# Row gathers of a sparse graph-attention layer, each block's first one made to wait for the sums three blocks back

## The chip, the core and the metric

The kernel runs on one core of one Trainium2 chip. A core has a matrix engine (TensorE, PE in the profile; its weight loads are PEld), VectorE (DVE), ScalarE (ACT), GpSimd (POOL) and SyncE (SP), each with its own queue of instructions[...]. The metric is the device time of one execution in microseconds (us).

## The reference

Two graph layers on 3327 nodes with 512 features; `adj` is a sparse 3327 x 3327 matrix whose first nodes have by far the most neighbours.

```python
h = relu(layernorm(x))
x = x + adj @ (relu(adj @ (h @ W1) + b1) @ W2) + b2          # layer 0
h = relu(layernorm(x))
t = adj @ h                                                   # layer 1
attn_a = sigmoid(concat([t, h]) @ Wa.T + ba)
attn_b = sigmoid(concat([t, h]) @ Wb.T + bb)
hs = h @ W_sa
scores = (hs @ a_left)[:, None] + (hs @ a_right)[None, :]
e = where(adj != 0, exp(-leaky_relu(scores, 0.01)), 0)
x_a = (e / (sum(e, axis=1) + 1e-5)) @ hs
x_b = adj @ (h @ W_gcnb) + b_gcnb
x = x + sigmoid(attn_a * x_a + attn_b * x_b)
```

## The kernel before

The nodes are padded to 26 blocks of 128 (NB = 26). Layer 0 reads the whole matrix twice, in chunks of 512 columns: once for `acc_u` (L511), once for `acc_g` (L665). Beside it the kernel lists, for every block but the first, which neighbours its nodes have, and GpSimd gathers the matrix's entries for these lists into `ae`. Layer 1's input rows are written to `h_dram` (L588).

Block 0 holds the hubs, whose rows are nearly dense: its two sums (with `adj` and with `e`) are made over all 26 blocks of rows, in `acc_hub`, by `add_hubs` (L619 to L639). The last product of these is the `add(1, NB - 1, ...)` of L639.

All other blocks are sparse. Block i has `rooms[i]` rooms: 3 for blocks 25 to 23, 4 for 22 to 11, 5 for 10 to 6, then 6, 6, 7, 8 and 10 for blocks 5 to 1. A room takes two indirect DMAs from GpSimd (L139, called from `attend`), each of 128 rows of `h_dram` (520 floats a row), so that a block of r rooms takes 2r row gathers, 238 in all. They land in a ring of 16 buffers, `rows` and `hr`, each of which holds one room; a buffer is free again when the products that read it are done. The blocks are taken from 25 down to 1. For block i the order of the work is:

- `attend(i)`: the row gathers on POOL; for each room an add of the two score parts on DVE (L780), then maximum, leaky part, exponential (ACT) and mask (L784 to L208), by segments of at most four rooms; the sum of the exponentials (L789).
- on PE, behind the step before: `weigh` of the block two steps back (p_b L863, p_a L870), `turn` of the block one step back (transposes L823, copied to `tyT` by DVE, L838), `add_es`, and `sums(i)` (L809), eight products per room.
- `copy_out(i)`: two copies of the sums to `ty` on ACT (L882, L886), which `turn` will read; `finish` of the block two steps back: L725 to L744 on DVE and ACT, and the store.

`weigh` starts with the hubs' block 0 after `sums(25)`. Its weights `W_g_sb` are loaded at the beginning of the stage (L711). The order on each engine is fixed by `queued` (an instruction is issued after those named); it makes no semaphore waits. Waits come from the data, from the ring's buffers, and from `pace`, which makes an instruction wait for a product. `attend` paces the first gather of a block:

```python
lead = LEAD[i < NB - 8]                                # LEAD = 3, 4
if k0 + k + q == 0 and len(combined) >= lead:
    pace(gathered[0], combined[-lead])
```

`combined` is the list of the last product of each `sums`. When block i is attended, its last entry is that of block i+1. So the first gathers of blocks 25 to 23 are not paced, those of 22 to 18 wait for the sums of block i+3, and those of 17 to 1 for the sums of block i+4. On a block of four rooms the ring of 16 buffers asks for block i+4 too.

Of the kernel before, what the change touches and what calls it, by code (L numbers as in the profile page):

```python
# [21 lines left out]
NQ = P // GW  # L22
HALF = P // 2
ROW = 520
LEAD = 3, 4
EH = 8
SEG = 4
WAKE = 30
# [18 lines left out]
def kernel(  # L47
# [17 lines left out]
    nc = tc.nc  # L65
    NP, D = x.shape
    HID = W1.shape[1]
    NB = NP // P
# [69 lines left out]
    def gather(dst, table, rows, last):  # L138
        return nc.gpsimd.indirect_dma_start(  # L139
            out=dst, out_offset=None, in_=table,  # L140
            in_offset=bass.IndirectOffsetOnAxis(ap=rows, axis=0),
            bounds_check=last, oob_is_err=False,
        )
# [21 lines left out]
    def pace(g, matmul):  # L165

        tc.add_manual_dep(
            g.ins, matmul.ins.name,
            mybir.DependencyInfo(mybir.DependencyClass.Sync, mybir.DependencyReason.DATA),
            reason="pace",  # L170
        )
# [7 lines left out]
    def queued(*insts):  # L179

        behind = ExitStack()
        for inst in insts:
            if inst is not None:
                behind.enter_context(tc.issue_after(inst.ins))
        return behind
# [18 lines left out]
    def masked_exp(e, adj):  # L204

        nc.vector.scalar_tensor_tensor(e, e, SLOPE, e, op0=ALU.mult, op1=ALU.max)  # L206
        done = nc.scalar.activation(e, e, AF.Exp, scale=-1.0)
        nc.vector.scalar_tensor_tensor(e, adj, 0.0, e, op0=ALU.not_equal, op1=ALU.mult)  # L208
        return done
# [6 lines left out]
    with (  # L216
# [402 lines left out]
        def add_hubs():  # L619

            def add(k, i, s):
                nc.tensor.matmul(  # L624
                    acc_hub[k], s, hrow[i % NR][:, :D], start=(i == 0), stop=(i == NB - 1)
                )

            for i in range(NB):
                while i not in rows_made:
                    yield  # L630
                add(0, i, a_hub[:, i, :])
                if i not in e_hub:
                    make_e_hub()
                yield
                if i:
                    add(1, i - 1, e_hub[i - 1])
                    e_added.add(i - 1)
                    yield
            add(1, NB - 1, e_hub[NB - 1])  # L639

        e_hub, e_added, last_e = {}, set(), [None, None]

        def make_e_hub():

            i = len(e_hub)
            if i not in rows_made or i - len(e_added) >= EH:
                return
            e = e_hub[i] = hubp.tile([P, P], F32, tag="e_hub", name=f"e_hub_{i}", bufs=EH)
            scores(e, s_hub, hrow[i % NR][:, D : D + 1])
            last_e[0] = masked_exp(e, a_hub[:, i, :])  # L650
            if i == 0:
                last_e[1] = nc.vector.tensor_copy(es_hub, e)
            else:
                last_e[1] = nc.vector.tensor_tensor(es_hub, es_hub, e, ALU.add)

        late, hubs = iter(()), add_hubs()
        QUIET = 6
        for c in range(NCH):
# [86 lines left out]
        return read_a, read_b  # L745

    with tc.tile_pool(name="spw", bufs=2) as spw:
        gathered, combined = [None], []
        own = [
            spw.tile([P, 2, ROW], F32, tag=f"hr{k}", name=f"hr{k}", bufs=1) for k in range(10)  # L750
        ]
# [4 lines left out]
        def attend(i, seg):  # L756


            r = rooms[i]
            k0, k1 = seg  # L760
            n = k1 - k0
            if k0 == 0:
                taken[i] = {"es": spw.tile([P, 2, GW], F32, tag="es", name=f"es_{i}")}
            es = taken[i]["es"]
            s_l = s_left[i * P // CW][:, i % (CW // P), :].rearrange("p (q i) -> p q i", q=2)
            both = ae[i][:, 2 * k0 : 2 * k1, :]
            e = both[:, :, GW:]
            hr = taken[i][k0] = []
            for k in range(n):
                hr.append(next(pairs))  # L770
                for q in range(2):
                    f = first[i] + q * r + k0 + k
                    with queued(gathered[0]):
                        gathered[0] = gather(
                            hr[k][:, q, :], h_dram[:, :], row_h[:, f : f + 1], NP - 1
                        )
                    lead = LEAD[i < NB - 8]
                    if k0 + k + q == 0 and len(combined) >= lead:
                        pace(gathered[0], combined[-lead])
                nc.vector.tensor_tensor(  # L780
                    e.rearrange("p (q k) i -> p k q i", q=2)[:, k],
                    s_l, hr[k][:, :, D : D + 1].to_broadcast([P, 2, GW]), ALU.add,
                )
            nc.vector.tensor_scalar(e, e, LEAST_SCORE, None, op0=ALU.max)  # L784
            exp = masked_exp(e, both[:, :, :GW])
            part = es
            if k0:
                part = spw.tile([P, 2, GW], F32, tag="part", name=f"part_{i}_{k0}")
            last = nc.vector.tensor_reduce(  # L789
                part, e.rearrange("p (q k) i -> p q i k", q=2), axis=AX.X, op=ALU.add  # L790
            )
            if k0:
                last = nc.vector.tensor_tensor(es, es, part, ALU.add)
            return last, exp
# [98 lines left out]
        with queued(last_e[1]):  # L893
            for seg in segments(NB - 1):
                made = attend(NB - 1, seg)
# [22 lines left out]
        for i in range(NB - 2, 1, -1):  # L918
            with queued(*held):
                for seg in segments(i):  # L920
                    made = attend(i, seg)
            if i == NB - 2:
                some_logits(2, made[0])
            with queued(added):
                added, add_es, end = weigh(*weighing)
            b, ty, es = turning
            with queued(added):
                tyT, added, copied = turn(b, ty, False)
            with queued(added):
                added = add_es()  # L930
            held = [copied, *end()]
            weighing = b, tyT, es
            with queued(added):
                for seg in segments(i):
                    added = sums(i, seg)
            combined.append(added)
            ty, last = copy_out(i, taken[i]["acc"])
            held.append(last)
            turning = i, ty, taken[i]["es"]

        segs = segments(1)
        with queued(*held):
            attend(1, segs[0])
# [26 lines left out]
    with tc.If(over > 0):  # L970
        with (
# [25 lines left out]
            for c in range(NCH):  # L997
# [34 lines left out]
                for b in range(w // P):  # L1032
                    i = c0 // P + b
# [63 lines left out]
```

## Time and profile before

| | |
|---|---|
| four runs | 855.86, 857.12, 859.83, 859.48 us; median 858.3 |
| the profiled execution's own time | 861.97 us |
| its span, first to last instruction | 860.2 us |
| mean granted TensorE clock | 0.971 |
| start of the first row gather | 461.98 us |
| last row gather starts | 815.2 us |
| row gathers: number, median length of a row | 238, 1002 ns |
| PE busy, POOL busy | 797.6 us (93%), 512.9 us (60%) |

A row of POOL's timeline gives the start and the length of one gather as GpSimd's own work, and in brackets how long POOL stood idle before it and which event came last before it started. A row of PE may merge several products, with their number. Start times are counted from the first instruction of the span.

### The profile page before, as it was taken

The page shows a single profiled execution, that of the slowest core. Times are in us where ns is not written, and L with a number is a line of the kernel's source. Part 1 is how long each engine was busy: PE and PEld are TensorE (multiplying, and loading weights), DVE is VectorE, ACT ScalarE, POOL GpSimd, SP SyncE. Part 2 cuts the span into 40 slices and gives each one's busy share as a digit, 9 for nine tenths or more (in the row PEclk, how much of TensorE's full clock was granted, in tenths as well). Part 3 has the DMA queues.
Part 4 walks back from the last instruction along what each step waited for, and adds up shares of the span by engine and source line. Part 5 has one row for each costly group of instructions (what it writes and reads, how often), then busy time and mean ns, then how long its engine had stood idle before and what let it go on. Part 6 is the DMA issues. An engine that isn't in the chain of part 4 may idle for free.

```text
span 860.2 us, 12424 instructions
## 1 busy us (share of the span) xinstructions
PE 797.6 (93%) x3707; PEld 427.5 (50%) x3707; DVE 519.4 (60%) x1668; ACT 188.3 (22%) x396; POOL 512.9 (60%) x533
## 2 busy tenths in 40 slices
PE   9999899999798999999999499799999999999795
PEld 8774444444543444444454365456564555454354
DVE  6778899998645776586565465354453535344342
ACT  6770000000002233033042121122221212112112
POOL 2303666666677776676664766767676767677500
PEclk9999999999799899999999799899999999999898
DMA  7787998897688998999956668878877777877620
GB/s 243 241 282 217 314 311 241 278 284 225 172 268 278 318 325 297 314 319 299 314 176 222 179 184 238 242 195 227 227 218 222 207 230 206 230 198 209 181 68 29
DMA packets 108219, 202.82 MB, mean 236 GB/s; under 512 B 17489, under 2 KB 31344, under 8 KB 108144
## 3 DMA queue, kind: packets, MB, share of 16 engines
q1 hardware_dynamic: 72800, 124.40, 44.4%
q0 software_dynamic: 26656, 66.41, 29.5%
q10 hardware_dynamic: 8688, 11.15, 3.9%
q8 instruction: 31, 0.51, 0.3%
q14 instruction: 44, 0.36, 0.1%
HBM read 182.22 MB, written 20.55 MB: 236 GB/s over the span
## 4 chain that ended last, share of the span: by engine, by line
PE 72%; DVE 9%; DMA 7%; issue 7%; POOL 1%; ACT 1%; SPq 1%; another core or an unknown queue 0%; POOLq 0%; DVEq 0%; ACTq 0%
PE acc L809 13%; PE acc_u L511 13%; PE p_b L863 11%; PE acc_g L665 11%; PE p_a L870 10%; DMA a<-in_adjT_dram 4%; PE pu L293 3%; PE ptt L823 3%; DVE most L515 2%; DMA xb<-in_x_dram 2%; PE p_list L459 2%; PE acc_hub L624 1%; DMA hr<-h_rows,row_h 1%; PE px L580 1%; PE pt L285 1%
## 5 line engine op out<-in xcount | busy, mean ns | idle before, releaser
L139 POOL DMA_INDIRECT ae<-in_adjT_dram,row_a x238 | 254.5, 1069 | 166.2 <-issue 64.3
L139 POOL DMA_INDIRECT hr<-h_rows,row_h x150 | 155.1, 1034 | 67.8 <-issue 34.7
L511 PE MATMUL acc_u<-a,rows 128*128 128x512 f32 (+1 forms) x364 | 167.3, 589 | 1.9 <-issue 1.2
L665 PE MATMUL acc_g<-a,g 128*128 128x512 f32 (+1 forms) x364 | 159.0, 575 | 8.1 <-DMA a<-in_adjT_dram 8.0
L139 POOL DMA_INDIRECT rows<-h_rows,row_h x88 | 90.9, 1033 | 53.1 <-issue 19.5
L863 PE MATMUL p_b<-W_g_sb,tyT 128*128 128x257 f32 x416 | 103.8, 396 | 16.9 <-issue 16.0
L515 DVE TENSOR_REDUCE most<-a 128x16 f32<-128x512 f32 (+1 forms) x182 | 112.1, 643 | 7.6 <-DMA a<-in_adjT_dram 4.3
L665 PEld LDWEIGHTS acc_g<-a,g 128*128 128x128 f32 x364 | 69.0, 195 | 87.0 <-issue 64.8
L863 PEld LDWEIGHTS p_b<-W_g_sb,tyT 128*128 128x128 f32 x416 | 78.7, 194 | 50.6 <-issue 24.9
L870 PE MATMUL p_a<-W_sa_sb,tyT 128*128 128x512 f32 (+2 forms) x216 | 94.7, 581 | 0.8 <-issue 0.8
L809 PE MATMUL acc<-hr,ae 64*64 64x512 f32 x600 | 86.5, 614 | 4.1 <-issue 3.4
L511 PEld LDWEIGHTS acc_u<-a,rows 128*128 128x128 f32 x364 | 65.6, 197 | 49.5 <-issue 43.2
L838 DVE COPY tyT<-ptt 128x512 f32<-128x512 f32 x51 | 34.9, 686 | 64.8 <-PE ptt L823 26.4
L870 PEld LDWEIGHTS p_a<-W_sa_sb,tyT 128*128 128x128 f32 x216 | 41.2, 191 | 40.8 <-issue 39.2
L809 PE MATMUL acc<-rows,ae 64*64 64x512 f32 x352 | 53.6, 596 | 3.3 <-DVE ae L206 1.9
L809 PEld LDWEIGHTS acc<-hr,ae 64*64 64x64 f32 x600 | 35.3, 137 | 39.3 <-issue 37.5
L208 DVE SCALAR_TENSOR_TENSOR ae<-ae 128x256 f32<-128x256 f32 (+2 forms) x36 | 12.8, 378 | 64.9 <-issue 32.6
L728 ACT ACTIVATE f<-f 128x2 f32<-128x2 f32 x26 | 5.3, 204 | 185.8 <-DVE f L727 70.2
L302 ACT ACTIVATE gT<-acc_u,b_col 128x512 f32<-128x512 f32 (+1 forms) x7 | 4.6, 657 | 164.0 <-PE acc_u L511 81.2
L696 DVE TENSOR_TENSOR xb<-xb,b_row 128x512 f32<-128x512 f32 x26 | 17.8, 690 | 34.0 <-DMA xb<-in_x_dram 32.8
L559 DVE SCALAR_TENSOR_TENSOR junk<-rows,w_rows 128x512 bf16<-128x512 f32 x52 | 35.7, 686 | 1.7 <-ACT rows L201 0.6
L823 PEld LDWEIGHTS ptt<-ident,ty 128*128 128x128 f32 x208 | 24.4, 142 | 19.4 <-issue 18.6
(142 smaller groups left out, 924.1 us busy)
## 6 DMA issues: line engine op xcount, KB each, us to landing
a<-in_adjT_dram SPq DMA_DIRECT2D x325, 256.0 KB
h_rows<-rows SPq DMA_DIRECT2D x26, 260.0 KB
x<-in_x_dram SPq DMA_DIRECT2D x26, 256.0 KB
xb<-in_x_dram SPq DMA_DIRECT2D x26, 256.0 KB
x<-xb ACTq DMA_DIRECT2D x26, 256.0 KB
x1b<-x SPq DMA_DIRECT2D x26, 256.0 KB
out_dram<-va SPq DMA_DIRECT2D x25, 256.0 KB
ae<-in_adjT_dram,row_a POOLq DMA_INDIRECT x238
```

What stands on the lines that cost most here:

```text
L139: return nc.gpsimd.indirect_dma_start(out=dst, out_offset=None, in_=table, in_offset=bass.IndirectOffsetOnAxis(ap=rows, axis=0), bounds_ch ...
L293: nc.tensor.matmul(pu[:, :HID], hT[:, k, :], W1_sb[:, k, :], start=(k == 0), stop=(k == KD - 1))
L511: added = nc.tensor.matmul(acc[:, :w], u[j], a[:, :w], start=(j == 0), stop=(j == NB - 1))
L515: nc.vector.tensor_reduce(most[:, : w // GW, j], a[:, :w].rearrange("p (b i) -> p b i", i=GW), axis=AX.X, op=ALU.max, apply_absolute_value ...
L559: return nc.vector.scalar_tensor_tensor(junk, h, 1.0, w_rows[:, s, :], op0=ALU.mult, op1=ALU.mult, accum_out=into)
L665: added = nc.tensor.matmul(acc[:, :w], g[j], a[:, j % per, :], start=(j == 0), stop=(j == NB - 1))
L696: nc.vector.tensor_tensor(xs[i], xs[i], b2_row, ALU.add)
L809: added = nc.tensor.matmul(taken[i]["acc"][h][q * HALF : (q + 1) * HALF, :], both[half_p, q * n + k, :], taken[i][k0][k][half_p, q, :D], s ...
L823: moved = nc.tensor.transpose(pt[:, k * P : (k + 1) * P], ty[h][:, k * P : (k + 1) * P], ident)
L838: last = nc.vector.tensor_copy(dst, src)
L863: nc.tensor.matmul(p_b[n][:, :WH], tyT[:, k, 0, :], W_g_sb[:, k, n * WH : (n + 1) * WH], start=(k == 0), stop=(k == KD - 1),)
L870: last = nc.tensor.matmul(p_a[:, c0:c1], tyT[:, k, 1, :], W_sa_sb[:, k, c0:c1], start=(k == 0), stop=(k == KD - 1),)
```

## The change

The first gather of every block from 24 to 1 is paced, with one lead of three. The list `combined` now begins with the hubs' last product: `add` returns its instruction and `add_hubs` appends the last one to `hubs_end`, which `combined` is. Blocks 24 and 23 wait for the hubs' last product (the list is shorter than three, or its third entry from the end is the hubs'), blocks 22 to 18 for the sums of block i+3 as before, and blocks 17 to 1 for the sums of block i+3 and no longer of i+4. Block 25 is not paced.

```diff
-LEAD = 3, 4
+LEAD = 3
...
             def add(k, i, s):
-                nc.tensor.matmul(
+                return nc.tensor.matmul(
                     acc_hub[k], s, hrow[i % NR][:, :D], start=(i == 0), stop=(i == NB - 1)
                 )
...
-            add(1, NB - 1, e_hub[NB - 1])
-
+            hubs_end.append(add(1, NB - 1, e_hub[NB - 1]))
+
+        hubs_end = []
...
-        gathered, combined = [None], []
+        gathered, combined = [None], hubs_end
...
-                    lead = LEAD[i < NB - 8]
-                    if k0 + k + q == 0 and len(combined) >= lead:
-                        pace(gathered[0], combined[-lead])
+                    if k0 + k + q == 0 and i < NB - 1:
+                        pace(gathered[0], combined[-min(LEAD, len(combined))])
```

## The prediction

> **What bounds the kernel now.** I read the engine totals and the chain of work that ended last, and then, because the change touches only the row gathers of the attention stage, the timelines of PE, POOL and ACT from 462 us on.
>
> ```profile
> PE 797.6 (93%) x3707; PEld 427.5 (50%) x3707; DVE 519.4 (60%) x1668; ACT 188.3 (22%) x396; POOL 512.9 (60%) x533
> PE 72%; DVE 9%; DMA 7%; issue 7%; POOL 1%; ACT 1%; SPq 1%; another core or an unknown queue 0%; POOLq 0%; DVEq 0%; ACTq 0%
> ```
>
> TensorE carries 72% of the chain, POOL 1%: a gather matters only through what it does to TensorE. Per block TensorE does p_b and p_a (7.1 us), transposes (1.0) and the sums of L809 (0.89 us per room), so a block of four rooms should take 11.8 us; the timeline gives 11.7 from the sums of block 22 to those of 21, and 11.7 from 19 to 18. In places it takes far more. First the PE timeline, then POOL's at the same places, then ACT's; the bracket is the engine's idle time before the row and what ended it.
>
> ```profile
> 477.78 1.09 PE L823 MATMUL ptt<-ident,ty 128*128 128x128 f32 x8
> 488.36 6.07 PE L863 MATMUL p_b<-W_g_sb,tyT 128*128 128x257 f32 x16 [9.49 <-issue]
> ...
> 547.59 1.14 PE L863 MATMUL p_b<-W_g_sb,tyT 128*128 128x257 f32 x4
> 549.02 0.38 PE L863 MATMUL p_b<-W_g_sb,tyT 128*128 128x257 f32 x1 [0.30 <-issue]
> 549.74 0.38 PE L863 MATMUL p_b<-W_g_sb,tyT 128*128 128x257 f32 x1 [0.34 <-issue]
> ```
>
> ```profile
> 484.62 1.00 POOL L139 DMA_INDIRECT hr<-h_rows,row_h  x1 [0.30 <-issue]
> 487.79 1.00 POOL L139 DMA_INDIRECT hr<-h_rows,row_h  x1 [2.17 <-remote]
> ...
> 537.67 1.00 POOL L139 DMA_INDIRECT hr<-h_rows,row_h  x1 [1.79 <-remote]
> ...
> 548.13 1.00 POOL L139 DMA_INDIRECT rows<-h_rows,row_h  x1 [0.30 <-issue]
> ...
> 557.27 1.00 POOL L139 DMA_INDIRECT rows<-h_rows,row_h  x1 [0.30 <-issue]
> 560.72 1.00 POOL L139 DMA_INDIRECT rows<-h_rows,row_h  x1 [2.45 <-PE p_b L863]
> ```
>
> ```profile
> 537.73 0.57 ACT L882 COPY ty<-acc 128x512 f32<-128x512 f32 x1
> 560.44 0.59 ACT L882 COPY ty<-acc 128x512 f32<-128x512 f32 x1 [10.74 <-PE p_b L863]
> ```
>
> What to see: POOL starts a gather every 1.305 us (1.00 and 0.30 idle) until one waits for TensorE. I call the gathers between two such pauses a run. From 462.0 to 485.6 there are 18 in one run, and TensorE stands from 478.9 to 488.4; from 537.7 to 558.3 there are 16, and from 548.3 to 559.6 TensorE starts a product every 0.7 to 1.4 us in place of 0.22. All ten runs of eight (487.8 to 535.9 and 560.7 to 630.3) pass without such a stretch. Both slow stretches end when POOL pauses. Results come late too: block 21's sums, started by 535.7, are copied out at 537.7, block 20's, started by 547.7, only at 560.4, again in a pause. My reading, an inference from this timing and no record, is: **once a run is over about 8 us old, TensorE's completions reach the others only in POOL's next pause, and from about 10.5 us TensorE itself crawls at a quarter of its pace.** Runs of ten (693.9 to 751.5) cost it one to three steps of 0.7 us each; the run of 16 from 631.8 to 653.2 about 5 us; those of 12 and 13 to 805.3 about 2, 2 and 11.
>
> **What the Trainium skill says.** "Perfetto Trace Analysis", section "DMA Instruction — SWDGE (GPSIMD)", says that the row of such a DMA ends when its descriptors are written, not when data have landed. The trace agrees: rows of 1.00 us, while the chain has "468.58 4.07 DMA hr<-h_rows,row_h". "TensorE: Matmul & The Clock Gate", Part 1, says that an idle window of about 3.4 us drops the clock to half. The trace agrees: 0.50 granted from 485 to 490 us, after the 9.49 us hole. "SBUF — State Buffer", the paragraph on the "DVE blocks DMA" trap, lets VectorE hold up GpSimd's descriptors; here the longest row gather is 1525 ns against 1002, so that is small, and no page states the reverse hold-up of TensorE.
>
> **The change part by part.** No instruction is added or removed; POOL's order is the same. Only its waits for TensorE move, as a comparison of the two instruction lists shows: block 24's first gather gains one, block 17's gains one; the first gathers of blocks 16 to 1 wait a block later, and in blocks 10 to 1 the waits inside the block become fewer (block 9: the first and the last four gathers before, only the first after). A held gather holds all later row gathers, the only work queued behind it on POOL; behind these wait the adds of L780 on DVE, the exponential on ACT and the sums on PE. SP's and ACT's queues keep their order.
>
> 1. *Hub wait.* Block 25's six gathers end at 469.6, the hubs' last product at 473.1: block 24 starts at about 473.4 in place of 469.9. The pause resets the run, so the transposes of 477.8 to 478.6 report in time and TensorE goes on at 480.3 (two 0.7 us copies) in place of 488.4. (The weights W_g_sb, issued at 459.5, are needed there too; but ACT's and DVE's copies, which need none, also stood until 487.5.) But block 23 waits for the same product and 22 for block 25's sums (over by 477.8), so the run is now 6+6+8 = 20 gathers, 473.4 to 499.5. TensorE crawls from 484 to 500.7. In these 16.7 us, at the 14 products that the stretch from 548.35 shows in 12 us, some 20 products pass: p_a and transposes. The sums of block 24 then end near 504, against 501.6: **+2.5**. Ends: -8, if no crawl comes (the 9.49 us hole gone), and +6, if nothing passes in the crawl.
> 2. *Block 17.* Its gathers wait for block 20's sums and not 21's. Those end at 547.7, when block 18's run of eight ends; the wait lasts about 2.0 us, as at 537.67 (sums over at 535.7). The run of 16 is gone; block 19's sums end 11.8 us after block 20's, not 20.9: **-9.1**. Blocks 16 to 11 stay at runs of eight. The sums of block 13 so end at 639.6 + 2.5 - 9.1 = 633.0.
> 3. *Start of the long blocks.* Block 10's first gather waits for block 13's sums, 633.0 + 2.0 = 635.0; before, it waited for block 14's and went at 631.8: **+3.2** for POOL, although TensorE is 6.6 ahead. From here to the end there are 124 gathers, 124 x 1.305 = 162 us, and 12 pauses, 22.6 us, which make the 184.4 of before (631.8 to 816.2). A block of five rooms takes POOL 13.05 + 1.8 = 14.9 us and TensorE 12.7 plus the crawl of a run of ten, (13.05 - 10.5 + 1.2) x 2/3 = 2.5: 15.2. The two are locked, so TensorE loses its lead over these five blocks, where before it took 14.5 per block (668.4 to 740.7, in runs of 8 and 10). Pauses after: nine block starts and, by the remaining waits inside blocks 4 to 1, three to six more, 12 to 15 against 12: 0 to +5.4, I take **+1.7**. Ring waits on the sums two blocks back act from block 4 on in both kernels, so that the last 44.0 us, from 816.2 to the end, stay.
>
> Landing hides the later gathers: gathers of block 10 end 31 us ahead of its sums now and some 20 after, and need 4.1 us to land and about 2 for L780 to L208. If that cover went, each us of lateness would count in full.
>
> Sum: +3.2 + 1.7 = **+4.9** (the first two steps are inside the 3.2). Against the profiled execution's own 861.97 us (span 860.2 and 1.8 around it) that gives 866.9. The four runs have a median of 858.3, 3.7 below the profiled one, so I forecast 858.3 + 4.9, or **863.0**.
>
> **Rivals.**
> *TensorE keeps its lead.* If runs of ten cost it only 0 to 2 us, as at 679 to 751, it stays 6.6 us ahead, and block 9's start breaks the run of 16 at 631.8, for another 2 or 3: 858.3 - 8.6 = 849.7, faster. It decides if TensorE needs less than POOL's 14.9 us per block and still doesn't wait for rows. For it: the chain is TensorE's in this stage, and rows have 20 to 31 us in hand. Against it: fast products make the next wait pass early in a run, and the run goes on.
> *That last point in full.* If block 8's or 7's wait is met within the first 8 us of a run, two blocks of ten gathers join, and one more stall like that of 548 to 559 costs 9: 863 + 9 = 872. For it: block 23 and 17 do this before. Against: it sets TensorE back, so it comes once.
> *The waits say nothing.* The slow stretches may have another cause, only coincident with runs; then the stalls stay, waits shift by 2 us inside 20 us of slack, and the time is 859 +- 3. For it: no record ties the engines. Against: all ten runs of eight are clean.
>
> **How the numbers follow.** Forecast case 0.46, at 863, itself 858 to 868; lead kept 0.30; joined runs 0.13; no effect 0.11. One measurement of this kernel can tell about 0.5%, 4.3 us, from no change: under 854.0 is faster, over 862.6 slower. Faster: 0.25 of the lead case and 0.02 = 0.27. Slower: 0.25 of the forecast case, 0.13, 0.02 = 0.40. The rest 0.33. The range 850 to 871 takes in step 1's +6 and half of the lead case; it leaves out the rest of that and the upper part of joined runs, together under 0.2.
>
> **What would show it.** Right: a pause near 470 to 473 and then about 20 gathers in one run; block 24's sums ending near 504; no run of 16 at block 17 and ACT's copy of block 20 within 3 us; block 13's sums near 633 and block 10's first gather near 635; runs of ten with a few 0.7 us steps from there; last gather near 821. Wrong: no crawl in the first long run; TensorE at block 6 still 6 us ahead; long runs without slow products, which would end the reading as a whole.

## The result, and the profile after

The changed kernel takes 860.9 us (median of 34 runs, 853.2 to 868.2), the kernel before 858.7 us (55 runs, 851.3 to 868.7): a ratio of 1.002, 95% interval 1.0003 to 1.0038. That is +2.2 us, where the prediction's sum was +4.9; by the prediction's bound of 0.5% that is no change. The profiled execution of after took 858.16 us, with a span of 856.4; it lies 2.7 below its median, that of before 3.3 above its own. So I compare the two traces by what happens after their first row gather (461.98 before, 458.42 after). In this pair that part takes the same time within 0.2 us, so the traces don't show where the +2.2 of the medians lies; they show how the parts moved against each other.

Of the page of after, the engines' totals and the shares of the chain that ended last:

```profile
PE 795.2 (93%) x3707; PEld 429.7 (50%) x3707; DVE 520.7 (61%) x1668; ACT 187.7 (22%) x396; POOL 509.7 (60%) x533
PE 69%; DVE 11%; issue 8%; DMA 7%; ACT 1%; POOL 1%; SPq 1%; POOLq 0%; ACTq 0%; DVEq 0%
```

The sums hardly moved; the places did. POOL's timeline of after, at the hub wait, at the end of the first long run and at block 17 (start, length, and in brackets the idle time before the row and what ended it; `issue` means that the engine waited for nothing that the profile shows, `remote` that the profile finds no instruction of this core as the releaser):

```profile
465.06 1.00 POOL L139 DMA_INDIRECT hr<-h_rows,row_h  x1 [0.30 <-issue]
469.82 1.00 POOL L139 DMA_INDIRECT hr<-h_rows,row_h  x1 [3.75 <-PE acc_hub L624]
...
506.82 1.00 POOL L139 DMA_INDIRECT rows<-h_rows,row_h  x1 [0.30 <-issue]
510.51 1.00 POOL L139 DMA_INDIRECT rows<-h_rows,row_h  x1 [2.68 <-remote]
...
547.99 1.00 POOL L139 DMA_INDIRECT rows<-h_rows,row_h  x1 [1.80 <-PE acc L809]
...
559.84 1.00 POOL L139 DMA_INDIRECT rows<-h_rows,row_h  x1 [1.72 <-PE acc L809]
```

PE's timeline of after at the first of these places, and ACT's copy of block 20's sums at block 17:

```profile
488.71 3.73 PE L863 MATMUL p_b<-W_g_sb,tyT 128*128 128x257 f32 x16 [1.55 <-DVE tyT L838]
...
501.56 1.77 PE L809 MATMUL acc<-hr,ae 64*64 64x512 f32 x3 [0.74 <-issue]
509.64 2.94 PE L863 MATMUL p_b<-W_g_sb,tyT 128*128 128x257 f32 x6 [6.31 <-issue]
```

```profile
549.43 0.57 ACT L882 COPY ty<-acc 128x512 f32<-128x512 f32 x1
```

What to see: the new wait of 3.75 us is released by the hubs' product (`acc_hub`), and the 9.49 us hole that ended at 488.36 in before is now one of 1.55. But then 28 gathers run without a pause, from 469.82 to 507.8, and TensorE stands for 6.31 us until 509.64, inside POOL's next pause (507.8 to 510.51). At block 17 POOL now pauses (547.99), the run of 16 is two runs of eight, and block 20's sums are copied at 549.43, 2.3 us after they ended and not 12.7.

An account of POOL from its first row gather on, from the rows of its timeline (a pause is any idle time over 0.45 us between two row gathers):

| us | before | after | after - before |
|---|---|---|---|
| 238 rows and the short gaps between them | 310.87 | 308.56 | -2.3 |
| pauses up to block 10's first gather (12 of each) | 20.9 | 24.6 | +3.7 |
| later pauses (12 of each) | 22.5 | 22.5 | 0.0 |
| last gather's end to the span's end | 44.0 | 42.4 | -1.6 |
| sum | 398.2 | 398.0 | -0.2 |

The pauses are what the edited waits set directly: +3.7, about the hub wait's 3.75. Whether the shorter rows (-2.3) and the shorter tail (-1.6) are the change's doing or chance, one trace of each can't say. The gain of nine at block 17 is nowhere in the sum. Why is the subject of the experiments.

### The profile page after: what moved, and what is told of

Its sections match the earlier page's. It is cut to its first block, busy times and chain, and to the rows that moved or that the text cites. A ratio compares the mean times of both kernels' runs of the same rounds, so it can differ in the third digit from the quotient of the medians.

```text
span 856.4 us, 12393 instructions
## 1 busy us (share of the span) xinstructions
PE 795.2 (93%) x3707; PEld 429.7 (50%) x3707; DVE 520.7 (61%) x1668; ACT 187.7 (22%) x396; POOL 509.7 (60%) x533
## 4 chain that ended last, share of the span: by engine, by line
PE 69%; DVE 11%; issue 8%; DMA 7%; ACT 1%; POOL 1%; SPq 1%; POOLq 0%; ACTq 0%; DVEq 0%
PE acc L809 14%; PE p_b L863 12%; PE acc_g L666 11%; PE acc_u L511 10%; PE p_a L870 10%; DMA a<-in_adjT_dram 4%; DVE most L515 3%; PE pu L293 3%; PE ptt L823 2%; DMA xb<-in_x_dram 2%; PE p_list L459 2%; PE acc_hub L624 2%; PE pt L285 1%; PE px L580 1%; DVE junk L559 1%
## 5 line engine op out<-in xcount | busy, mean ns | idle before, releaser
L863 PE MATMUL p_b<-W_g_sb,tyT 128*128 128x257 f32 x416 | 105.8, 405 | 15.7 <-issue 12.0
L863 PEld LDWEIGHTS p_b<-W_g_sb,tyT 128*128 128x128 f32 x416 | 81.1, 201 | 48.4 <-issue 20.9
L809 PE MATMUL acc<-rows,ae 64*64 64x512 f32 x352 | 51.4, 596 | 5.7 <-issue 3.7
L809 PEld LDWEIGHTS acc<-rows,ae 64*64 64x64 f32 x352 | 20.3, 133 | 25.1 <-issue 21.1
```

The costliest lines, as they stand in the source:

```text
L809: added = nc.tensor.matmul(taken[i]["acc"][h][q * HALF : (q + 1) * HALF, :], both[half_p, q * n + k, :], taken[i][k0][k][half_p, q, :D], s ...
L863: nc.tensor.matmul(p_b[n][:, :WH], tyT[:, k, 0, :], W_g_sb[:, k, n * WH : (n + 1) * WH], start=(k == 0), stop=(k == KD - 1),)
```

## The experiments

They ran in seven sets, each on one chip together with runs of before. In five sets before took 791.9 to 792.6 us, in two 857.6 and 861.7, the level of the prediction. A run is compared with before in its own set only. I say "the 792 level" and "the 858 level"; the record doesn't tell what makes it, and the same chip number appears with both. Of the 69.2 us between the spans of before's two traces (860.2 and 791.0), 16.6 lie ahead of the first row gather (461.98 and 445.34), in layer 0, and no run here says why; the rest lies in the stage of the row gathers.

Theory C is the prediction's reading: long unbroken runs of row gathers hold TensorE up. Theory R, formed after the result, is: POOL's stretch (238 gathers at 1.305 us, plus pauses) sets when the last rows come, and with that the end, so a pause costs about its length and TensorE's gains in the middle are worth nothing. Theory T: TensorE's chain sets the end, and POOL has slack. Theory X: TensorE is slow at the 858 level whatever POOL does. In the expectations of the first set, "theory R" still stands for C and R together.

**One part of the change alone.** First the hub wait, then the lead of three.

```diff
-            add(1, NB - 1, e_hub[NB - 1])
+            hubs_end.append(add(1, NB - 1, e_hub[NB - 1]))
...
-                    if k0 + k + q == 0 and len(combined) >= lead:
-                        pace(gathered[0], combined[-lead])
+                    if k0 + k + q == 0 and i < NB - 1:
+                        pace(gathered[0], combined[-min(LEAD[i < NB - 8], len(combined))])
```

> Only the hub wait of the change: blocks 24 and 23 wait for the hubs' last product, every other block keeps the lead of before (3 for blocks 22 to 18, 4 below). Theory R (long unbroken runs of gathers hold TensorE up, and the stage's end follows POOL's gathers and pauses): the first run is about 28 gathers, the run of 16 at blocks 18 and 17 stays, block 22's sums end about 3 us later after the start of the first gather than before; the time is 2 to 4 us above before. Theory T (TensorE's own chain sets the end, and TensorE goes on earlier to the hubs' p_b): 0 to 8 us below before.

Measured: 797.0, ratio 1.0057 (1.0036 to 1.0078).

```diff
-LEAD = 3, 4
+LEAD = 3, 3
```

> Only the lead of the change: three for every block, blocks 24 and 23 unpaced as before. Theory R: the run of 18 at the start stays, the run of 16 at block 17 goes, block 13's sums end 9 us earlier, block 10's first gather starts within 1 us of before's time, and the rest follows it: 0 to 4 us below before. Theory T: TensorE keeps the 9 us, 7 to 10 us below before.

Measured: 796.4, ratio 1.0059 (1.004 to 1.0078). The hub wait is 0.6 us over R's range. The lead of three misses both theories: it is 4.0 us above before, where R had it 0 to 4 below and T 7 to 10 below. Both expectations had been worked out from the traces of the 858 level, but the runs came at the 792 level, and so did these repetitions, which were meant for the other:

> Only the wait for the hubs' last product at block 24. Where before takes 858: the pause of 3.8 us adds to POOL; the first run of 18 becomes a longer one. By the prediction's first step +2.5 for TensorE and, with POOL's later waits locked to TensorE, +2.5 at the end (0 to +4); if the broken run removed the 9.5 us hole, -5 or less. Where before takes 792: +4.6 again.

> Only the wait for the hubs' last product. Where before takes 858: +2.5 (0 to +4) by the prediction's first step, if what POOL loses at block 24 is carried to the end; 0 or less, if the 9.5 us hole goes with it. Where before takes 792: +3 to +4.6.

> Only the lead of three for blocks 17 to 1, no hub wait. Where before takes 858: POOL's account (number and length of pauses; all other terms equal) expects the first run of 18 and its hole as in before, the run of 16 at block 17 gone, block 10 started by TensorE's sums of block 13, and in all one pause more for block 17 and none saved: 0 to +2 us. If TensorE's 9.2 us at block 17 came through to the end: -5 to -9. Where before takes 792: +4 again.

> Only the lead of three for blocks 17 to 1, without the hub wait. Where before takes 858: if POOL's pauses set the end, 0 to +2 us, with the first run of 18 as in before, the run of 16 at block 17 gone and TensorE's gain there given back by block 6; if TensorE's 9.2 us at block 17 came through to the end, -5 to -9. Where before takes 792: +4 to +6.

Measured: hub wait 795.1, ratio 1.003 (1.0009 to 1.0051), and 796.4, ratio 1.005 (1.0028 to 1.0071); lead 798.5, ratio 1.0076 (1.0056 to 1.0095), and 797.1, ratio 1.0064 (1.0043 to 1.0084). What follows stands below, with the whole change. What either part does alone at the 858 level was not measured.

**The whole change, before itself, and no pacing.** Before and the changed kernel were run as they are; the third drops the pacing:

```diff
-                    if k0 + k + q == 0 and len(combined) >= lead:
+                    if k0 + k + q == 0 and len(combined) >= 99:
```

> The kernel before, for its trace beside the others. On the chip of the first four experiments (before: 792.4 us) theory R, that POOL's gathers pace the end, expects all 238 gathers in one run of 238 x 1.305 = 310.6 us with no pause over 0.5 us, TensorE without a slow stretch, and about 792. On the chip of the prediction (before: 858.7 us) it expects the pauses of the first trace: a run of 18, runs of 8, a run of 16.

> The changed kernel. On the chip where before takes 792.4: theory R (POOL's gathers and pauses pace the end) expects the hub wait of 3.8 us, and of the later waits only what TensorE is behind by then: lead alone gave 4.7 us of pauses, but POOL now comes 3.8 later and TensorE about 1 later, so 1.5 to 2.5 remain: 792.4 + 3.8 + 2 = 798 (797 to 800). Theory T (TensorE's chain paces the end, POOL has slack) expects 792.4 + 1 = 793.5. On the chip where it takes 858.7: 860 to 862, as first measured.

> No gather is paced; only the ring's buffers hold one back. On the chip where before takes 792.4, no wait of before ends last, so both R and T expect no change, 792 +- 1. On the chip where it takes 858.7: theory C (TensorE is held up during long unbroken runs of gathers, and POOL's pauses release it) expects longer runs and with them more holes, slower by 5 to 30 us; theory X (the slow stretches have another cause, pauses only cost POOL time) expects up to 5 us faster.

Measured at the 792 level: before's own trace 792.75 (a single run); the changed kernel 798.1, ratio 1.0063 (1.0039 to 1.0087); no pacing 792.95, ratio 1.001 (0.999 to 1.0029). A table by stretches of before's trace: length, then for each engine its busy time and number of instructions, TensorE's clock, the DMA share:

```profile
500.00:560.00 60.00, 60.00 (x346) 36.30 (x345) 32.40 (x103) 15.38 (x34) 46.28 (x46) 1.00 0.84 247
560.00:620.00 60.00, 60.00 (x348) 36.49 (x347) 30.70 (x100) 13.98 (x30) 46.28 (x46) 1.00 0.83 252
620.00:680.00 60.00, 60.00 (x367) 36.59 (x366) 34.25 (x129) 14.70 (x35) 45.97 (x47) 1.00 0.83 242
```

What to see: TensorE is busy for 60.00 of 60.00 us while POOL issues 46 gathers in each stretch; all 238 follow each other from 445.3 to 760.9 without a pause. So theory C doesn't hold here: in these stretches, inside a run of 238, TensorE has no hole. POOL's three pauses in the changed kernel, from its timeline:

```profile
458.83 1.00 POOL L139 DMA_INDIRECT hr<-h_rows,row_h  x1 [3.81 <-PE acc_hub L624]
...
593.64 1.35 POOL L139 DMA_INDIRECT hr<-h_rows,row_h  x1 [0.81 <-PE acc L809]
...
605.31 1.51 POOL L139 DMA_INDIRECT hr<-h_rows,row_h  x1 [1.07 <-PE acc L809]
```

Their sum is 5.69 us and the kernel is 5.8 slower. It holds for the others of this level too (the pauses are of one execution each, the times are medians):

| kernel | pauses in its trace | time against before |
|---|---|---|
| no pacing | 0 | +0.6 |
| hub wait (three runs) | 3.78, 3.78, 3.77 | +4.6, +3.0, +3.9 |
| lead of three (three runs) | 4.66, 7.30, 5.16 | +4.0, +6.4, +4.6 |
| the whole change | 5.69 | +5.8 |

So R is right at the 792 level, T is not, and the parts don't add up: with the hub wait POOL comes later to the waits behind it, and of the four to seven pauses that the lead of three makes alone, two are left.

**More gathers, and cheaper ones.** Each block from 24 on gets one gather more, into a buffer that nothing reads; and the row gathers lose the bound on their indices.

```diff
+            if k0 == 0 and i < NB - 1:
+                spare = spw.tile([P, ROW], F32, tag="spare", name=f"spare_{i}", bufs=1)
+                with queued(gathered[0]):
+                    gathered[0] = gather(
+                        spare, h_dram[:, :], row_h[:, first[i] : first[i] + 1], NP - 1
+                    )
```

> Before with one more row gather per block for blocks 24 to 1, into a spare buffer that nobody reads: 24 gathers of 1.305 us, 31 us of POOL. Theory R (POOL's gathers and pauses pace the stage): 20 to 35 us above before. Theory T: POOL idles 44 us of the 354 between its first and last row gather, the extra work goes there: less than 6 us above before.

```diff
-            bounds_check=last, oob_is_err=False,
+            **({} if last is None else dict(bounds_check=last, oob_is_err=False)),
...
-                            hr[k][:, q, :], h_dram[:, :], row_h[:, f : f + 1], NP - 1
+                            hr[k][:, q, :], h_dram[:, :], row_h[:, f : f + 1], None
```

> The row gathers are issued without a bound on their indices (those of the matrix's entries keep theirs). If the bound costs GpSimd time, a gather starts more often than every 1.305 us, and R expects 238 times the difference off the end of POOL's stretch, until TensorE's own chain, about 2 us below, is the limit. If it costs nothing, the cadence stays at 1.305 us and the time is as before. I expect no change, 0 +- 2 us.

> Row gathers without a bound, with before's waits. Where before takes 858: gathers of 1.253 in place of 1.305 us, 238 x 0.052 = 12.4 us less issue; but POOL's pauses there are locked to TensorE, so at most the share between the pauses of the long blocks comes through: -3 to -8. If runs hold TensorE by their number and not their time, 0. Where before takes 792: -6 again.

Measured at the 792 level: 24 more gathers 823.0, ratio 1.0396 (1.0342 to 1.045), +30.6, as 24 x 1.305 = 31.3. Without the bound 786.3, ratio 0.9922 (0.9893 to 0.9951), and again 786.9, ratio 0.9937 (0.9913 to 0.996): I had expected nothing. The chain's shares by engine with the extra gathers:

```profile
PE 49%; DMA 28%; DVE 9%; issue 6%; POOL 4%; ACT 3%; POOLq 0%; SPq 0%; DVEq 0%; ACTq 0%
```

The same in before at this level:

```profile
PE 77%; DMA 10%; DVE 8%; issue 2%; ACT 2%; POOL 1%; SPq 0%; POOLq 0%; DVEq 0%; ACTq 0%
```

A gather without the bound, on POOL's timeline:

```profile
605.19 0.95 POOL L139 DMA_INDIRECT rows<-h_rows,row_h  x1 [0.30 <-issue]
```

Before at this level, ahead of block 2's sums, on PE's and DVE's timelines:

```profile
737.33 1.93 PE L823 MATMUL ptt<-ident,ty 128*128 128x128 f32 x8 [2.23 <-ACT ty L882]
```

```profile
735.25 0.22 DVE L780 TENSOR_TENSOR ae<-s_left,hr 128x64 f32<-128x64 f32 x1 [2.56 <-DMA hr<-h_rows,row_h]
```

PE's timeline at the same place without the bound:

```profile
731.97 1.04 PE L823 MATMUL ptt<-ident,ty 128*128 128x128 f32 x8
```

A row of 0.95 in place of 1.00 makes a start every 1.253 us, and POOL's stretch 305.1 in place of 315.6 us. In before TensorE waits at 737.33 for ACT's copy to `ty`. ACT issues it only after a step (L742) that waits for DVE (L740), and DVE is held by the adds of L780, which wait for rows (735.25). Without the bound TensorE doesn't wait there, and only 6 of these 10.5 us come through to the end; my reading is that the end passes from POOL to TensorE there. So the chain gives POOL 1% in before, and yet POOL's number of gathers sets the end; with the extra ones the wait shows, as 28% DMA.

**The same waits where POOL has slack.** The changed kernel, and the hub wait alone, both without the bound (the edits are those shown).

> The changed kernel with row gathers issued without a bound. With before's waits this form ran at 786.3 us: its gathers start every 1.253 us, POOL ends its last gather 13.4 us earlier than in before, and TensorE sets the end. Theory R (the end is the later of TensorE's chain and POOL's last gather + 12.8 us, and the waits bind POOL to TensorE): hub wait 3.8 us, then the waits at blocks 13 to 10 hold POOL to TensorE's 11.7 us per block where its own eight gathers take 10.0: block 10 starts 10.8 later than without the change, last gather about 758.3, last sums 771.1 in place of 764.3: +6.8, 793. Theory T (POOL has slack now, so waits cost only what they delay TensorE itself, 1.8 us by the late first blocks): 788.

> Only the hub wait of the change, with row gathers issued without a bound. With the bound this wait cost 4.6 us (797.0 against 792.4). R: POOL's 3.8 us now lie inside the 6 us by which it is ahead of TensorE at the end, and only the 1.8 us that TensorE's first blocks lose remain: 786.3 + 1.8 = 788 (787 to 789). If a pause of POOL costs its length wherever it stands: 786.3 + 4.6 = 791.

Measured at the 792 level: 793.9, ratio 1.0026 (1.0002 to 1.005), and 787.9, ratio 0.9949 (0.993 to 0.9969). Against the 786.3 without these waits (from another set, so to about 1 us) that is +7.6 and +1.6. Both are R's numbers, 793 and 788: the hub wait, 4.07 us here, costs less than half of its length where POOL is ahead; with the lead of three added the headway is gone (six pauses, 11.38 us in all).

**No gathers at all.** The row gathers become plain transfers of one fixed block of rows each, issued by SP; so other rows than the graph's are read, and the loads and stores that SP issued go to GpSimd.

```diff
-                        gathered[0] = gather(
-                            hr[k][:, q, :], h_dram[:, :], row_h[:, f : f + 1], NP - 1
+                        j = (f * 7) % NB
+                        gathered[0] = nc.sync.dma_start(
+                            hr[k][:, q, :], h_dram[j * P : (j + 1) * P, :]
                         )
...
-        nc.sync.dma_start(x1, x1_dram[i])
+        nc.gpsimd.dma_start(x1, x1_dram[i])
...
-            nc.sync.dma_start(out[i * P : (i + 1) * P, c0:c1], a)
+            nc.gpsimd.dma_start(out[i * P : (i + 1) * P, c0:c1], a)
```

> The row gathers leave GpSimd: each is a plain DMA from SyncE of 128 fixed rows of h_dram, with the same bytes, the same buffers and the same pacing as before, so the attention reads rows other than the listed ones; GpSimd issues the loads of x1 and the stores instead. Theory R with GpSimd's issuing as the cause: no products 0.7 us apart, ACT's copies of a block's sums within 1 us of them, periods of four-room blocks 11.8 us and of five-room blocks 12.7 us, and block 1's sums end 40 to 55 us earlier than before, the time 800 to 825 us. If the bytes on the DMA engines are the cause (the same 63 MB): slow stretches as before and the time within 10 us of before.

> The 238 row gathers become plain transfers of a fixed block of rows each, issued by SP, with the same bytes and the same waits; other rows than the graph asks for are read, and GpSimd issues the loads of x1 and the stores instead. Where before takes 858: theory C (POOL's long runs of gathers hold TensorE up) expects no slow stretch after 470 and the stage as short as on the chips where before takes 792 (346 us in place of 398): about 807 to 815. Theory X (TensorE is slow on this chip whatever POOL does) expects 850 or more. Where before takes 792: no change again, 795.

> The plain transfers in place of the row gathers once more, for a chip where before takes 858: theory C expects 807 to 815 and no slow stretch after the first block; theory X 850 or more. Where before takes 792: 795.

Measured at the 792 level: 795.0, ratio 1.0014 (0.9992 to 1.0037), and 794.1, ratio 1.0022 (0.9993 to 1.0051); the first expectation, 800 to 825, had been worked out from the 858 level. This is no evidence for T: DVE's last result is ready at 780.4 in place of 785.5 (the first of the two profiled executions against before's trace), and then the last store, now issued by GpSimd, takes 13.0 us to the end of the span (793.4) in place of 5.5 (791.0). At the 858 level, where there is a single run of each: **805.4 us against 861.7** for before beside it, just under theory C's 807 to 815 and far outside the spread of before's 55 runs at this level (851.3 to 868.7). Its table by stretches:

```profile
500.00:560.00 60.00, 60.00 (x345) 36.30 (x345) 30.99 (x102) 13.99 (x30) 5.93 (x12) 1.00 0.78 267
560.00:620.00 60.00, 60.00 (x346) 36.25 (x345) 30.34 (x100) 13.99 (x30) 5.36 (x10) 1.00 0.72 240
620.00:680.00 60.00, 60.00 (x363) 36.66 (x362) 33.01 (x123) 14.57 (x34) 5.36 (x10) 1.00 0.74 244
```

No slow stretch is left in these 180 us. That this run was at the 858 level its own trace shows: the hubs' last product ends at 470.1, in before's traces at 473.1 (858 level) and 456.2 (792 level). From there to the end of block 1's sums it takes 309.2 us, where before takes 369.6. At the 792 level the same stage takes 310.3 (the second of the two runs) and in before 317.5. So without the row gathers the stage is the same at both levels, and theory X is out. The 56 us, 6.5%, are what the row gathers cost there. Which side of a gather costs them is not shown: the edit takes away GpSimd's issuing and, with it, the scattered rows; 238 plain transfers issued by GpSimd were not run.

**Long runs at the 858 level.** No pacing and no bound together (both edits as shown), so that only the ring's 16 buffers hold POOL back.

> No gather is paced, and the row gathers carry no bound: POOL runs as far ahead as the 16 buffers allow. Where before takes 792: TensorE sets the end already in the form with before's waits (786.3), and those waits held nothing, so 786 +- 1.5 again; if a free POOL's transfers disturbed TensorE, 788 or more. Where before takes 858 (the chip of the prediction): theory C (long runs of gathers hold TensorE up) expects fewer pauses and longer slow stretches, slower than before by 5 to 30 us; if the slow stretches have nothing to do with runs, about 12 us faster.

Measured: 875.5 against 857.6, ratio 1.0176 (1.0113 to 1.024), +17.9. At the 792 level no pacing had cost nothing and the missing bound had given 6. Neither was run alone at the 858 level, so what each has in the 17.9 is open. PE's, POOL's, ACT's and DVE's timelines at the first run, of 28 gathers from 466.3 to 502.2:

```profile
482.16 1.09 PE L823 MATMUL ptt<-ident,ty 128*128 128x128 f32 x8
506.51 5.94 PE L863 MATMUL p_b<-W_g_sb,tyT 128*128 128x257 f32 x13 [23.26 <-DVE tyT L838]
```

```profile
501.21 0.95 POOL L139 DMA_INDIRECT rows<-h_rows,row_h  x1 [0.30 <-issue]
509.15 0.95 POOL L139 DMA_INDIRECT rows<-h_rows,row_h  x1 [6.99 <-DVE a_hub L566]
```

```profile
499.44 0.59 ACT L882 COPY ty<-acc 128x512 f32<-128x512 f32 x1 [19.52 <-remote]
```

```profile
505.77 1.29 DVE L838 COPY tyT<-ptt 128x512 f32<-128x512 f32 x2 [23.02 <-remote]
```

What to see: the transposes end at 483.2. DVE, idle since 482.75, starts their copy only at 505.77, 3.6 us after POOL's last gather of the run ended; block 25's sums, over by 482.2, are copied at 499.44. Between 483.2 and 499.4 none of these three starts anything, while POOL issues. ACT's copy needs nothing from DVE, so DVE alone is not what was held. This is theory C at its plainest, at this level only. It isn't as strict as the prediction had it: ACT's copy came 2.7 us ahead of POOL's pause. The long runs cost most at the beginning: counted from the first gather, block 22's sums end 24.2 us later than in before (86.3 and 62.1), block 1's 11.2 later (391.9 and 380.7).

## Why the prediction was wrong in size

*Step 1, the hub wait: right in its wait, and in its size by luck.* The pause is 3.75 us (3.8 forecast) and starts, counted from the first gather, where it should. The hole of 9.49 us is gone, as forecast. What follows went another way. Block 24's sums end 28.8 us after the first gather, in before 39.6; the forecast was 42.0. So block 21's wait for them was met when it came up, and the next run has 28 gathers and not 20. And the crawl set in near 499, 29 us into the run, not after 10.5: a fixed age of the run at which TensorE slows was read out of too few places. The later crawl and the hole of 6.31 us then took the gain back: block 22's sums end 65.3 us after the first gather in place of 62.1, +3.2. That this is near the forecast of +2.5 for block 24 is chance.

*Step 2, block 17: right.* Block 19's sums end 11.6 us after block 20's (558.7 and 547.1) in place of 20.9; block 13's end 7.1 us earlier, relative to the first gather (forecast 6.6).

*Step 3, first half: right.* Block 10's first gather starts 173.0 us after the first one in place of 169.9: +3.2, as forecast; since this is the sum of the first two steps and the wait, it has step 1's luck in it. TensorE gives its lead back: from block 13's sums to block 6's it takes 111.4 us (628.9 to 740.3), before 101.1 (639.6 to 740.7), so the rival that it keeps its lead is out. It gives it back by crawling, not by waiting for rows: of its waits from 640 to 741, 11.1 us are put down to `issue` and 0.4 to DVE. PE's timeline of after in the run of ten from 660.81:

```profile
670.80 0.38 PE L863 MATMUL p_b<-W_g_sb,tyT 128*128 128x257 f32 x1 [0.84 <-issue]
671.53 0.38 PE L863 MATMUL p_b<-W_g_sb,tyT 128*128 128x257 f32 x1 [0.35 <-issue]
672.24 0.48 PE L863 MATMUL p_b<-W_g_sb,tyT 128*128 128x257 f32 x1 [0.33 <-issue]
```

The 858-level answer to "where did the gain at block 17 go" is this: block 10's gathers now wait for block 13's sums where they had waited for block 14's, so POOL starts its last 124 gathers no earlier, and TensorE, ahead of them, loses its lead in their runs. It rests on the two traces; the lead alone was measured only at 792.

*Step 3, second half: the step that failed.* "Pauses after: ... 12 to 15 against 12: 0 to +5.4, I take **+1.7**". There are 12 of 22.5 us, in after as in before: 0.0. The lower end of the bound was right, and I took a third of the way up with no view that carried it. The last gather so starts 354.6 us after the first, before 353.2; the forecast of 821 was 359.0. Without this term the sum is +3.2, just inside the interval of the measured ratio (0.3 to 3.3 us). "The last 44.0 us ... stay" was off by -1.6 in this pair of executions. Counted from the first gather, block 3's sums still end 3.4 us later than in before, and block 2's 0.2 earlier: the slow stretch between them is 3.6 us shorter. Whether the change or chance made that, one trace of each can't say. A slip of the sum besides: 858.3 + 4.9 is 863.2, not 863.0.

*The reading as a whole.* That gathers hold TensorE up is borne out at the 858 level by taking them away (-56 us, one run), and that the length of their runs matters by letting the runs grow (+17.9, with the bound gone as well). That "a gather matters only through what it does to TensorE", from POOL's 1% of the chain, was too strong: at the 792 level the same POOL with the same 1% sets the end by its mere number of gathers, and there the change costs 5.8 us by that way alone. What separates the two levels stays open: the gathers' length and spacing are the same, 1.00 and 0.30 us, in both.

The version that beats both is before's waits with row gathers without a bound, at the 792 level (786.3 and 786.9). At the 858 level it was not run with before's waits.

## What to carry to other kernels

Where an engine issues a fixed number of long instructions and the work waits for the last of them, keep its account (number times interval, plus pauses, plus the tail) beside the chain of waits: a wait that is added ahead of it can cost its length even if its share of the chain is 1%, and a stall removed in the consumer gives nothing unless the producer starts earlier. Before adding a wait, ask whether the producer has slack: here the same wait cost 3.0 to 4.6 us without it and 1.6 with it. And where no view says where in its bound a term lies (here 0 to +5.4), keep the bound in the forecast and don't take a point from its inside.

## What was not expected of the hardware

- At the 858 level, while GpSimd issued indirect DMAs without a pause, finished transposes reached DVE 22.5 us late (483.2 to 505.77), and plain transfers by SP in place of these DMAs took 56 us less; at the 792 level 238 in a row left TensorE busy for 60.00 of 60.00 us in three stretches.
- Without the bound on the indices an indirect DMA of 128 rows takes 0.95 us on GpSimd in place of 1.00, with 0.30 between two in both cases.
- A last store issued by GpSimd ended the span 13.0 us after its data were ready, one issued by SP 5.5.
